# Two gather tables for the expert blocks: one with the first row alone, one with both

## The chip, the cores and the metric

The kernel runs on one core of one Trainium2 chip. The metric is device time in microseconds (us): the median of three runs for the kernel as it stands, and beside it the time of one profiled execution, from which all durations below come. Engines are named as in the profile: PE (TensorE), PEld (its weight loads), DVE (VectorE), ACT (ScalarE), POOL (GpSimd) and SP (SyncE, which here only issues DMAs). Everything is float32.

## The reference, cut to what matters

The input x has two rows (sequences) of 1024 tokens with 256 channels. Four residual steps follow each other: a conditioned state-space block with an MLP, a pooled mixture of 16 experts, a differential attention, and a top-1 mixture of 8 experts. The change touches the second:

```
h = pooled(x)               # per row: masked softmax pooling; every token reads tokens of its own row
logits = -|h - key_e|^2 + h . rw_e + rb_e          # 16 experts
topv, topi = top_k(logits, 4);  w = softmax(topv)
x = x + sum_k w_k * ( gelu(h @ w1[topi_k].T + b1) @ w2[topi_k].T + b2 )
```

Nothing in this step mixes tokens of the two rows. What a token needs for its experts is its own pooled row h (256 numbers) and its 16 expert weights (four of them not zero).

## The kernel before, in words

**Stages.** For each row b there are three pieces ahead of the experts:

- `mlp(b)` (lines 558 to 577): the MLP of the first residual step, 64 matmuls of 512 columns (L564) with a Gelu on ACT (L568) and 128 matmuls of 256 columns (L572). It leaves x in the tile `X[b]` and copies it to the DRAM table `acc[0]` (L575).
- `pooling(b)` (579 to 718): transposes of X (L585), scores (L594, Tanh L595, L599), two running maxima over 1024 tokens on DVE (L615, L616), exponentials on ACT (L653, L640, L664), the far part of the sums (L679) and a loop over eight tiles of tokens (L684, L685 on PE, L687 to L689 on DVE, L692 on ACT) that gives the pooled rows `pl`. Two DMAs write `pl` to the DRAM table `prow` (L694). Then the logits and the choice of the four experts (L702 to L718).
- `slots(s)` (743 to 860): sorts (token, expert) pairs into blocks of 256 slots that have one expert each. Counts are summed on PE (L758, L760), and one-hot matmuls (L832) turn slots into token numbers, which end in `idx[s]` (L860); `exi[s]` holds the expert of each block, `whose[s]` its mask. Within it, `weights_of(s)` (720 to 732) computes the expert weights of row s and writes them into the last 16 columns of `prow` (L730).

`slots(0)` sees row 0 alone. It fills up to eight blocks (`NB1`) with row 0's pairs, full blocks only. `slots(1)` sees both rows, leaves out what the first eight blocks hold, and fills the others. The program text has the order mlp(0), pooling(0), slots(0), mlp(1), pooling(1), slots(1), then the blocks.

**The expert blocks** (907 to 987). 36 blocks run always (`NB0`): eight of `s = 0`, then 28 of `s = 1`; further ones stand behind a condition. For each, `fetch` (910) loads the expert's weights, 2052 KB (L915), and its bias (L917) from SP, and POOL gathers 2 x 128 rows of `prow` into `gx` (L922). `turned` (928) transposes them (L933) and copies them to SBUF (L935). `block` (938) does 32 + 32 matmuls of 256 columns (L951 into `mm`, two PSUM banks; L963 into `o`) with a Gelu on ACT between them (L952), weighs the result (L959 to L966) and adds it into `acc` with an indirect DMA (L967). Weights have three buffers, `gx` four. The weights lie where the MLP weights lay (`block1.close()`, L895), so the first load waits for the last matmul of mlp(1).

**What sets the order.** The framework records all instructions with their dependencies, tile by tile, and orders each engine's queue when the kernel is built: it walks a model of the engines' times and takes, of what the model says is ready, the instruction that stands first in the program text. So mlp(1), which stands behind slots(0), fills the gaps that pooling(0) and slots(0) leave on PE. On the chip each queue then runs strictly in that order. A dependency on a DRAM table is kept for the range of it that an instruction names: the gather at L922 names all of `prow`, since the rows it takes are only known at run time.

```
            for h in range(2):
                pool.indirect_dma_start(
                    out=gx[:, h], out_offset=None, in_=prow,
                    in_offset=bass.IndirectOffsetOnAxis(ap=idx[s][:, 2 * j + h : 2 * j + h + 1], axis=0),
                )
```

`prow` has 2048 + 128 rows; the last 128 are zeros for slots that hold no pair (L889).

Of the kernel before, what the change touches and what calls it, by code (L numbers as in the profile page):

```python
# [11 lines left out]
F32 = mybir.dt.float32  # L12
# [7 lines left out]
P = 128  # L20
B, L, D = 2, 1024, 256
NT = L // P
NH, HP, NS = 8, 64, 64
DI = NH * HP
E0, F0, TOPK = 16, 1024, 4
# [50 lines left out]
def forward(ctx, tc, a):  # L76
    nc = tc.nc
# [3 lines left out]
    dram = ctx.enter_context(tc.tile_pool(name="dram", bufs=1, space=DRAM))  # L81
# [39 lines left out]

    ytab = dram.tile([B * L + P, 2 * D], F32, tag="ytab", name="ytab")

    prow = dram.tile([B * L + P, D + E0], F32, tag="prow", name="prow")
    acc = [dram.tile([B * L + P, D], F32, tag=f"acc{h}", name=f"acc{h}") for h in range(2)]


# [87 lines left out]
    with block0, tc.tile_pool(name="aps", bufs=2, space=PSUM, reuse_waits="tile") as ps:  # L215
# [21 lines left out]
        for b in range(B):  # L237
# [7 lines left out]
            for g in range(2):  # L245
                cols = slice(g * 512, (g + 1) * 512)
                p = ps.tile([P, 512], F32, tag=f"mm{b}", name="mm")
# [3 lines left out]
            for m in range(2):  # L251
                for g in range(2):
                    cols = slice(g * 512, (g + 1) * 512)
                    p = product(b, "Wg", both, m, cols)
                    act.activation(gated[b][:, m, cols], p, AF.Sigmoid, bias=C["bg"][:, m : m + 1])
                    pool.tensor_mul(gated[b][:, m, cols], gated[b][:, m, cols], xT[:, m, cols])
                    if m == 0:
                        for d in range(2):
                            p = ps.tile([P, 512], F32, tag=f"mm{b}", name="mm")
                            pe.matmul(  # L260
                                p, lhsT=C["Wn2"][:NS, d : d + 1].to_broadcast([NS, P]), rhs=h1[b][:, cols],
# [19 lines left out]
        for b in range(B):  # L281
            for g in range(2):
                cols = slice(g * 512, (g + 1) * 512)
                for m in range(2):
                    p = product(b, "Wsoma", [xTs[b][:, k] for k in range(2)], m, cols)
                    act.activation(soma[b][:, m, cols], p, AF.Gelu, bias=C["bsoma"][:, m : m + 1])
            for g in range(2):
                cols = slice(g * 512, (g + 1) * 512)
                for m in range(2):
                    p = product(b, "Wtemp", [ema[b][:, k] for k in range(2)], m, cols)  # L290
# [5 lines left out]
            for i in range(NT):  # L296
                p = ps.tile([P, D], F32, tag=f"o{b}", name="o")
                for k in range(2):
                    pe.matmul(
                        p, lhsT=soma[b][:, k, i * P : (i + 1) * P], rhs=WA["Wout"][:, k], start=k == 0, stop=k == 1  # L300
# [43 lines left out]
    with tc.tile_pool(name="b1", bufs=1, reuse_waits="tile") as bp:  # L344
# [4 lines left out]
        with tc.tile_pool(name="b2", bufs=2, reuse_waits="tile") as cp, tc.tile_pool(  # L349
            name="b3", bufs=1, reuse_waits="tile"  # L350
        ) as sp_, tc.tile_pool(
            name="bps", bufs=2, space=PSUM, reuse_waits="tile"
        ) as ps:
            for b in range(B):
# [27 lines left out]
                for g in range(2):  # L382
                    p = ps.tile([P, 512], F32, tag="mm", name="mm", bufs=3)
# [31 lines left out]
                t = taps(raw, C["bcw"])  # L415
# [3 lines left out]
                for c in range(4):  # L419
                    projected(xs[b][:, c], 512 + c * P)  # L420
                    t = taps(xs[b][:, c], C["cw"][:, c])
                    act.activation(xs[b][:, c, 3 : L + 3], t, AF.Silu, bias=C["cb"][:, c : c + 1])
                for i in range(NT):
                    p = ps.tile([P, 512], F32, tag="mm", name="mm", bufs=3)
                    for k in range(2):
                        pe.matmul(
                            p, lhsT=hT[:, k, i * P : (i + 1) * P], rhs=inp[:, k, 0:DI], start=k == 0, stop=k == 1
# [5 lines left out]
        with tc.tile_pool(name="b5", bufs=1, reuse_waits="tile") as sp, tc.tile_pool(  # L433
            name="b6", bufs=2, reuse_waits="tile"
        ) as tp, tc.tile_pool(name="bp1", bufs=2, space=PSUM, reuse_waits="tile") as p1, tc.tile_pool(
            name="bp2", bufs=1, space=PSUM, reuse_waits="tile"
# [6 lines left out]
            for b in range(B):  # L443
                vec.tensor_mul(av[b], dt[b], negA.unsqueeze(1).to_broadcast([P, NT, NH]))

                for dst, mat in ((ecs, K["U"]), (esuf, K["SL"]), (etot, ones)):
                    p = p2.tile([P, NT, NH], F32, tag="g", name="pg")
# [4 lines left out]
            for i, b in [(i, b) for i in range(NT) for b in range(B)]:  # L452
# [10 lines left out]
                for q in range(2):  # L463
                    p = p1.tile([P, 4, P], F32, tag="seg", name="seg")
# [114 lines left out]
    def pooling(b, cp, ps):  # L579
        xT = cp.tile([P, 2, L], F32, tag="xT", name="xT")  # L580
        for g in range(2):
            for k in range(2):
                t = ps.tile([P, 512], F32, tag="mm", name="tr")
# [5 lines left out]
        s, pre, suf = (cp.tile([P, L], F32, tag=t, name=t) for t in ("s", "pre", "suf"))  # L589
        for g in range(2):  # L590
            cols = slice(g * 512, (g + 1) * 512)
            p = ps.tile([P, 512], F32, tag="mm", name="mm")
# [5 lines left out]
            p = ps.tile([P, 512], F32, tag="mm", name="mm")  # L598
# [77 lines left out]
        pl = cp.tile([P, NT, DX], F32, tag="xT", name="pl")  # L676
        p = ps.tile([P, DX], F32, tag="mm", name="pf")
# [4 lines left out]
        for j in range(NT):  # L682
            p = ps.tile([P, DX], F32, tag="mm", name="po")
# [7 lines left out]
            n = b * NT + j  # L691
            act.activation(junk, pl[:, j, 0:D], AF.Square, accum_out=xsq[:, n : n + 1])  # L692
        for q in range(2):
            nc.sync.dma_start(  # L694
                out=prow[b * L + q * 512 : b * L + (q + 1) * 512, 0:D].rearrange("(i p) c -> p i c", p=P),
                in_=pl[:, 4 * q : 4 * q + 4, 0:D],
            )


        mine = slice(b * NT, (b + 1) * NT)  # L700
        lg_, gt_, eq_, rank_, wt_, ngt_ = lg[:, mine], gt[:, mine], eq[:, mine], rank[:, mine], wt[:, mine], ngt[:, mine]
# [18 lines left out]
    def weights_of(b):  # L720

        mine = slice(b * NT, (b + 1) * NT)
        wt_, ngt_ = wt[:, mine], ngt[:, mine]
        vec.tensor_sub(wt_, lg[:, mine], over_e(m8[:, mine, 0], half))
        act.activation(wt_, wt_, AF.Exp)
        vec.tensor_mul(wt_, wt_, gt[:, mine])
        vec.tensor_reduce(ngt_, wt_, AX.X, ALU.add)
        vec.reciprocal(ngt_, ngt_)
        vec.tensor_mul(wt_, wt_, over_e(ngt_, half))
        nc.sync.dma_start(  # L730
            out=prow[b * L : (b + 1) * L, D:].rearrange("(i p) c -> p i c", p=P), in_=wt_
        )

# [126 lines left out]
    with tc.tile_pool(name="cs", bufs=3, space=PSUM, reuse_waits="tile") as cs:  # L862
        with ExitStack() as c0:
            cp0 = c0.enter_context(tc.tile_pool(name="c0", bufs=1, reuse_waits="tile"))
            with tc.tile_pool(name="m1", bufs=2, side="right", reuse_waits="tile") as tp, tc.tile_pool(
                name="mps", bufs=2, space=PSUM, reuse_waits="tile"
            ) as ps:
                p = ps.tile([P, 512], F32, tag="mm", name="mm")
                for k in range(2):
                    pe.matmul(p[:, :E0], lhsT=ones, rhs=ksq[:, k], start=k == 0, stop=k == 1)  # L870
                vec.tensor_sub(rowb, R["rb"], p[:, :E0])
                h2 = [tp.tile([P, 2, L], F32, tag=f"h2{b}", name="h2", bufs=1) for b in range(B)]
                for b in range(B):
                    layernorm_T(h2[b], xa[b], C["ln2w"], C["ln2b"], tp, ps)
                for b in range(B):
                    x, wide = X[b][:, :, 0:D], [P, NT, D]
                    vec.tensor_add(x, x, xa[b])
                    vec.tensor_add(x, x, R["mb2"].unsqueeze(1).to_broadcast(wide))

                zero = tp.tile([P, 4 * D], F32, tag="zero", name="zero", bufs=1)  # L880
                pool.memset(zero, 0.0)
                for t, rows in ((acc[1], B * L),):
                    for q in range(rows // (4 * P)):
                        nc.sync.dma_start(
                            out=t[q * 4 * P : (q + 1) * 4 * P, :].rearrange("(i p) c -> p i c", p=P),
                            in_=zero.rearrange("p (i c) -> p i c", i=4),
                        )
                for t in (prow, ytab, *acc):
                    nc.sync.dma_start(out=t[B * L :, :], in_=zero[:, : t.shape[1]])  # L889
                mlp(0, tp, ps, h2[0])  # L890
                pooling(0, cp0, cs)
                with tc.tile_pool(name="d1", bufs=1, reuse_waits="tile") as cp:
                    slots(0, cp, cs)
                mlp(1, tp, ps, h2[1])
# [12 lines left out]
        with tc.tile_pool(name="fps", bufs=2, space=PSUM, reuse_waits="tile") as ps:  # L907
            got = {}

            def fetch(q):  # L910

                s, j = q
                e = nc.sync.value_load(exi[s][0:1, j : j + 1], min_val=0, max_val=E0 - 1)
                w = wpool.tile([P, FW], F32, tag="w", name="w")
                nc.sync.dma_start(out=w, in_=a["f0w"][bass.ds(e, 1)].rearrange("o p c -> p (o c)"))  # L915
                b2 = tp.tile([P, D], F32, tag="b2", name="b2", bufs=3)
                nc.sync.dma_start(  # L917
                    out=b2, in_=a["f0b2"][bass.ds(e, 1), :].rearrange("o c -> (o c)").partition_broadcast(P)
                )
                gx = tp.tile([P, 2, D + E0], F32, tag="gx", name="gx", bufs=4)  # L920
                for h in range(2):
                    pool.indirect_dma_start(  # L922
                        out=gx[:, h], out_offset=None, in_=prow,
                        in_offset=bass.IndirectOffsetOnAxis(ap=idx[s][:, 2 * j + h : 2 * j + h + 1], axis=0),
                    )
                got[q] = w, b2, gx
# [61 lines left out]
        with tc.tile_pool(name="d4", bufs=2, reuse_waits="tile") as tp:  # L988
            for b in range(B):
                nc.sync.dma_start(  # L990
                    out=X[b][:, :, 0:D], in_=acc[0][b * L : (b + 1) * L, :].rearrange("(i p) c -> p i c", p=P)
# [11 lines left out]
    with tc.tile_pool(name="e1", bufs=1, reuse_waits="tile") as cp, tc.tile_pool(  # L1003
        name="e2", bufs=2, reuse_waits="tile"
    ) as tp, tc.tile_pool(name="e3", bufs=1, reuse_waits="tile") as up_, tc.tile_pool(
        name="fs", bufs=2, space=PSUM, reuse_waits="tile"
    ) as p_s, tc.tile_pool(name="ft", bufs=1, space=PSUM, reuse_waits="tile") as p_t, tc.tile_pool(
        name="fm", bufs=2, space=PSUM, reuse_waits="tile"
# [255 lines left out]
    with tc.tile_pool(name="h1", bufs=1) as cp, tc.tile_pool(name="h2", bufs=2) as tp, tc.tile_pool(  # L1264
        name="hw", bufs=3
# [13 lines left out]
        with tc.tile_pool(name="i1", bufs=2) as up_, tc.tile_pool(name="i2", bufs=1) as ip, tc.tile_pool(  # L1279
            name="ips", bufs=2, space=PSUM  # L1280
        ) as ps:
            pg = ps.tile([P, N, E1], F32, tag="pg", name="pg", bufs=1)
            for b in range(B):
# [14 lines left out]
                for i in range(NT):  # L1298
                    p = ps.tile([P, D], F32, tag="o", name="o")
# [3 lines left out]
                for q in range(2):  # L1303
                    nc.sync.dma_start(
                        out=ytab[b * L + q * 512 : b * L + (q + 1) * 512, 0:D].rearrange("(i p) c -> p i c", p=P),
                        in_=yN[:, 4 * q : 4 * q + 4],
# [4 lines left out]
                for g in range(2):  # L1311
                    p = ps.tile([P, 512], F32, tag="o", name="o")
# [78 lines left out]
        with tc.tile_pool(name="jps", bufs=2, space=PSUM) as ps:  # L1391
# [27 lines left out]
            for e in range(E1):  # L1419
# [4 lines left out]
                gx, b2, dT = got.pop(e)  # L1424
                hh = tp.tile([P, 8, CAP], F32, tag="hh", name="hh")
                for f in range(8):
                    p = ps.tile([P, CAP], F32, tag="mm", name="mm", bufs=3)
# [5 lines left out]
                for s, n in parts:  # L1433
                    p = ps.tile([P, D], F32, tag="o", name="o")
                    for f in range(8):
# [7 lines left out]
                        out=a["out"].rearrange("b l c -> (b l) c"),  # L1443
                        out_offset=bass.IndirectOffsetOnAxis(ap=idx2[:n, col], axis=0),
                        in_=eo[:n], in_offset=None, bounds_check=B * L - 1, oob_is_err=False,
# [119 lines left out]
```

## Time and profile before

| | us |
|---|---|
| median of three runs (lowest, highest) | 1718.36 (1716.95, 1719.16) |
| the profiled execution, its own time | 1722.24 |
| its span in the trace | 1720.5 |
| busy in the span: PE, PEld, DVE, ACT, POOL | 1586.1, 1085.9, 783.1, 569.7, 350.0 |
| mean granted PE clock | 0.943 |

The page gives the busy time of each engine, then the span in 40 slices of 43 us; a digit is the busy share of a slice in tenths, 9 being 90% or more. In the row PEclk it is the clock that PE was granted, in tenths of the full one. Ends of matmuls are modelled, so a PE that counts as busy need not be at its peak. A table by stretches gives the same for stretches of one's own choice, with counts in brackets. A line of the waits names the instruction that waited, what ended its wait, the total, the number of times and the longest.

### The profile page before, as it was taken

Reading aid. Unit: us, or ns where it says so; the run is one execution under the profiler, and the core shown is the slowest. Engines: PE = TensorE matmul, PEld = TensorE weight load, DVE = VectorE, ACT = ScalarE, POOL = GpSimd, SP = SyncE. Lnnn points to the kernel's source line nnn. Section 1 sums busy time; section 2 is a strip of 40 time slices with the busy share of each in tenths; the row PEclk is TensorE's granted clock in tenths of the full one; section 3 lists DMA queues with packets and bytes.
Section 4 is the critical chain, followed back from the end, with each engine's and each line's share of the span. In section 5 each row is a group of like instructions: output and inputs, shape, how many; then the busy total and the mean of one; then the engine's idle time right before and its main releaser. Section 6 shows DMA issues by size and latency. Waiting matters only on the chain. (4 is left out here: it accounts for less than half of the span.)

```text
span 1720.5 us, 17699 instructions
## 1 busy us (share of the span) xinstructions
PE 1586.1 (92%) x6478; PEld 1085.9 (63%) x6478; DVE 783.1 (46%) x1854; ACT 569.7 (33%) x1146; POOL 350.0 (20%) x275
## 2 busy tenths in 40 slices
PE   8989999779997799999999999679999998859998
PEld 2444566546463688888888888535556554547775
DVE  6957666671645922222222222158755675231111
ACT  4556433221412122222222222116655564102221
POOL 2100355200000233333333332211000000022321
PEclk9989999979897799999999999889999998869999
DMA  5000000030006166666666665310000100443430
GB/s 197 1 1 0 1 1 0 1 114 25 25 2 233 53 191 195 195 196 195 194 194 194 194 194 175 67 52 1 1 1 1 50 0 1 165 134 122 163 107 11
DMA packets 54751, 156.79 MB, mean 91 GB/s; under 512 B 7819, under 2 KB 41867, under 8 KB 47488
## 3 DMA queue, kind: packets, MB, share of 16 engines
q1 hardware_dynamic: 38144, 128.86, 21.3%
q0 software_dynamic: 16512, 26.73, 7.5%
q8 instruction: 52, 0.85, 0.2%
q14 instruction: 43, 0.35, 0.1%
HBM read 130.74 MB, written 25.44 MB: 91 GB/s over the span
## 5 line engine op out<-in xcount | busy, mean ns | idle before, releaser
L952 ACT ACTIVATE hh<-mm,w 128x256 f32<-128x256 f32 x288 | 136.3, 473 | 398.7 <-PE mm L951 398.7
L951 PE MATMUL mm<-gT,w 128*128 128x256 f32 x1152 | 258.1, 382 | 0.8 <-DVE gT L935 0.8
L963 PE MATMUL o<-w,hh 128*128 128x256 f32 x1152 | 256.1, 379 | 0.0
L951 PEld LDWEIGHTS mm<-gT,w 128*128 128x128 f32 x1152 | 208.9, 191 | 42.9 <-ACT hh L952 2.6
L963 PEld LDWEIGHTS o<-w,hh 128*128 128x128 f32 x1152 | 215.7, 190 | 27.4
L967 POOL DMA_INDIRECT acc<-eo,idx x72 | 114.5, 1591 | 193.5 <-DVE wr L960 169.6
L922 POOL DMA_INDIRECT gx<-prow,idx x72 | 72.1, 1001 | 384.9 <-DVE nblk L778 224.8
L1151 PE MATMUL s<-kT,qz 128*128 128x512 f32 (+3 forms) x384 | 143.4, 495 | 5.2 <-DVE nm L1163 4.8
L935 DVE COPY gT<-t 128x512 f32<-128x512 f32 x36 | 24.9, 692 | 207.5 <-PE t L933 207.5
L1170 ACT ACTIVATE e<-e,nm 128x384 f32<-128x384 f32 (+7 forms) x128 | 98.7, 772 | 50.6 <-DVE nm L1163 49.5
L965 DVE TENSOR_TENSOR eo<-o,b 128x256 f32<-128x256 f32 x72 | 30.6, 425 | 180.2 <-PE o L963 180.2
L1163 DVE CUSTOM_DVE_ANT_0 e<-s,zneg 128x384 f32<-128x384 f32 (+7 forms) x128 | 95.3, 753 | 34.1 <-PE s L1151 29.8
L1151 PEld LDWEIGHTS s<-kT,qz 128*128 128x128 f32 x384 | 64.5, 190 | 48.0 <-issue 27.6
L1436 PE MATMUL o<-w,hh 128*128 128x256 f32 (+1 forms) x384 | 86.1, 382 | 0.0
L1436 PEld LDWEIGHTS o<-w,hh 128*128 128x128 f32 (+1 forms) x384 | 65.0, 172 | 18.3 <-issue 2.7
L1429 PE MATMUL mm<-dT,w 128*128 128x320 f32 x256 | 73.8, 448 | 0.5 <-DVE dT L193 0.5
L1430 ACT ACTIVATE hh<-mm,cols 128x320 f32<-128x320 f32 x64 | 33.7, 527 | 115.4 <-PE mm L1429 115.4
L1201 PE MATMUL po<-dT,vv 128*128 128x512 f32 (+3 forms) x192 | 68.3, 509 | 0.0
L1192 PEld LDWEIGHTS t<-consts,e 128*128 128x128 f32 x288 | 36.9, 149 | 45.3 <-ACT dT L193 15.8
L1090 POOL TENSOR_TENSOR sq<-qT 128x512 f32<-128x512 f32 x8 | 8.4, 1044 | 275.5 <-DVE qT L193 110.4
L1429 PEld LDWEIGHTS mm<-dT,w 128*128 128x128 f32 x256 | 49.6, 196 | 23.5 <-issue 4.7
L564 PE MATMUL mm<-h,wb 128*128 128x512 f32 x128 | 60.4, 618 | 0.4 <-ACT hh L568 0.4
(776 smaller groups left out, 2383.4 us busy)
## 6 DMA issues: line engine op xcount, KB each, us to landing
w<-in_f0w SPq DMA_DIRECT2D x36, 2052.0 KB, 8.7
w<-in_f1w SPq DMA_DIRECT2D x16, 1024.0 KB, 5.0
b<-in_f0b SPq DMA_DIRECT2D x36, 128.0 KB, 9.1
wb<-in_wb SPq DMA_DIRECT2D x1, 2560.0 KB, 17.5
X<-in_x SPq DMA_DIRECT2D x2, 1024.0 KB, 6.8
acc<-zero SPq DMA_DIRECT2D x4, 512.0 KB, 8.4
acc<-X SPq DMA_DIRECT2D x2, 1024.0 KB, 8.4
prow<-pl SPq DMA_DIRECT2D x4, 512.0 KB, 3.0
```

The source lines that it names most:

```text
L564: pe.matmul(p, lhsT=WB["m1"][:, k, f * P : (f + 1) * P], rhs=h2[:, k, g * 512 : (g + 1) * 512], start=k == 0, stop=k == 1,)
L922: pool.indirect_dma_start(out=gx[:, h], out_offset=None, in_=prow, in_offset=bass.IndirectOffsetOnAxis(ap=idx[s][:, 2 * j + h : 2 * j + h ...
L951: pe.matmul(p, lhsT=w1[:, k, f * P : (f + 1) * P], rhs=gT[:, k], start=k == 0, stop=k == 1)
L952: act.activation(hh[:, f], p, AF.Gelu, bias=fb[:, f : f + 1])
L963: pe.matmul(p, lhsT=hh[:, f, h * P : (h + 1) * P], rhs=w2[:, f], start=f == 0, stop=f == 7)
L967: pool.indirect_dma_start(out=acc[h], out_offset=bass.IndirectOffsetOnAxis(ap=idx[s][:, 2 * j + h : 2 * j + h + 1], axis=0), in_=eo, in_of ...
L1151: pe.matmul(t[:, s0:s1], lhsT=qz[b, c, i // 2][:, 2 * hp + j, (i % 2) * P : (i % 2 + 1) * P], rhs=kT[b][:, c, s0:s1], start=True, stop=True,)
L1163: vec.tensor_tensor_reduce(out=e[:, :n], in0=ss.pop((s, u))[:, :n], in1=zneg[:, L - n :], scale=-1.0, scalar=3e38, op0=ALU.add, op1=ALU.mi ...
L1170: act.activation(e[:, :n], e[:, :n], AF.Exp, bias=nm, scale=-1.0, accum_out=r)
L1201: pe.matmul(po[:, at:], lhsT=vv[b][:, q, c, hp : hp + 2].rearrange("p h d -> p (h d)"), rhs=dT[hp, q // 4][:, q % 4, at:], start=q == 0 an ...
L1429: pe.matmul(p, lhsT=w1[:, k, f * P : (f + 1) * P], rhs=dT[:, k], start=k == 0, stop=k == 1)
L1436: pe.matmul(p[:n], lhsT=hh[:, f, s * P : s * P + n], rhs=w2[:, f], start=f == 0, stop=f == 7)
```

## The change

`prow` becomes two tables of the same shape. Row 0's pooled rows and weights are written to both, row 1's only to the second. Rows 1024 to 2047 of the first are filled with zeros at the start of the stage. A block of `s = 0` gathers from the first, a block of `s = 1` from the second.

```diff
-    prow = dram.tile([B * L + P, D + E0], F32, tag="prow", name="prow")
+    prow = [dram.tile([B * L + P, D + E0], F32, tag=f"prow{s}", name=f"prow{s}") for s in range(2)]
...
         for q in range(2):
-            nc.sync.dma_start(
-                out=prow[b * L + q * 512 : b * L + (q + 1) * 512, 0:D].rearrange("(i p) c -> p i c", p=P),
-                in_=pl[:, 4 * q : 4 * q + 4, 0:D],
-            )
+            for t in prow[b:]:
+                nc.sync.dma_start(
+                    out=t[b * L + q * 512 : b * L + (q + 1) * 512, 0:D].rearrange("(i p) c -> p i c", p=P),
+                    in_=pl[:, 4 * q : 4 * q + 4, 0:D],
+                )
...
-        nc.sync.dma_start(
-            out=prow[b * L : (b + 1) * L, D:].rearrange("(i p) c -> p i c", p=P), in_=wt_
-        )
+        for t in prow[b:]:
+            nc.sync.dma_start(out=t[b * L : (b + 1) * L, D:].rearrange("(i p) c -> p i c", p=P), in_=wt_)
...
-                for t in (prow, ytab, *acc):
+                nc.sync.dma_start(
+                    out=prow[0][L : B * L, :].rearrange("(i p) c -> p i c", p=P),
+                    in_=zero[:, : D + E0].unsqueeze(1).to_broadcast([P, NT, D + E0]),
+                )
+                for t in (*prow, ytab, *acc):
                     nc.sync.dma_start(out=t[B * L :, :], in_=zero[:, : t.shape[1]])
...
                     pool.indirect_dma_start(
-                        out=gx[:, h], out_offset=None, in_=prow,
+                        out=gx[:, h], out_offset=None, in_=prow[s],
```

## The prediction

> **What bounds the kernel now.** I read the page first, the rows of slices, to see where the TensorE (PE) is not at work.
>
> ```profile
> span 1720.5 us, 17699 instructions
> ...
> PE 1586.1 (92%) x6478; PEld 1085.9 (63%) x6478; DVE 783.1 (46%) x1854; ACT 569.7 (33%) x1146; POOL 350.0 (20%) x275
> ...
> PE   8989999779997799999999999679999998859998
> PEclk9989999979897799999999999889999998869999
> ```
>
> A slice is 43 us. From slice 15 to slice 25 (about 606 to 1100 us) lie the 36 expert blocks, with PE full at full clock. Slices 13 and 14 (516 to 602 us) show 7 and 7, at a clock of 7 and 7: that is where row 1 is pooled and its slots are computed. A table by stretches resolves it; the columns are PE, PEld, DVE, ACT, POOL busy, then clock, DMA share and GB/s. The second group is the same work for row 0, with the MLP of row 1 beside it.
>
> ```profile
> 519.00:528.00 9.00, 7.40 (x34) 2.90 (x33) 3.05 (x6) 3.24 (x6) 0.00 (x0) 0.99 0.89 291
> 528.00:544.00 16.00, 6.50 (x22) 2.64 (x22) 14.77 (x29) 3.31 (x4) 0.00 (x0) 0.58 0.98 380
> 544.00:558.00 14.00, 13.86 (x31) 5.89 (x29) 5.78 (x22) 3.56 (x14) 0.00 (x0) 0.66 0.27 93
> 558.00:574.00 16.00, 3.65 (x9) 2.06 (x10) 14.16 (x66) 2.10 (x4) 5.14 (x5) 0.50 0.25 69
> 574.00:606.00 32.00, 32.00 (x198) 28.22 (x199) 29.71 (x101) 3.79 (x8) 7.66 (x9) 0.92 0.13 38
> ...
> 420.00:440.00 20.00, 20.00 (x77) 10.18 (x77) 11.58 (x19) 6.92 (x11) 0.00 (x0) 1.00 0.15 52
> 440.00:460.00 20.00, 18.81 (x55) 8.48 (x53) 12.14 (x35) 10.71 (x20) 0.00 (x0) 0.82 0.08 27
> 460.00:480.00 20.00, 19.96 (x72) 13.30 (x71) 15.69 (x88) 5.27 (x9) 0.00 (x0) 0.84 0.10 29
> ```
>
> Row 0's chain costs PE almost no idle time, because other matmuls fill it; row 1's chain leaves PE idle and at half clock. Next, the waits of PE from 519 to 606 us, to see what it waits for:
>
> ```profile
> PE pf L679 <- DVE wf L654: 9.5, 1, 9.5
> PE t L933 <- DMA gx<-prow,idx: 6.6, 2, 5.6
> PE mm L758 <- DVE gt L716: 5.1, 1, 5.1
> ```
>
> Last, why the blocks of row 0, whose slots were ready at 491.3 us (first idx of L860), start at 570.6. The page says that the first gather waited for DVE's nblk (L778). The gather's own line, in three stretches, says otherwise; its semaphore waits end one by one:
>
> ```profile
> L922 POOLq EVENT_SEMAPHORE  x1: 43/43/43, 552.6 to 552.6; - x1
> ...
> L922 POOLq EVENT_SEMAPHORE  x1: 43/43/43, 561.8 to 561.8; - x1
> ...
> L922 POOLq EVENT_SEMAPHORE  x2: 43/43/43, 566.7 to 566.8; - x2
> L922 POOL DMA_INDIRECT gx<-prow,idx x1: 1140/1140/1140, 567.6 to 567.6; - x1
> ```
>
> Row 1's two writes of pooled rows were issued at 549.25 and 558.81 (about 3.0 to landing) and its weights at 564.50 (2.1): they land at 552.3, 561.8 and 566.6. These are the gather's waits. It reads only rows of row 0, but names the whole table.
>
> **What the change takes away.** The first table holds no write of row 1 but zeros of about 354 us, so the eight gathers of row 0 need only writes of 454 to 475 us. The next thing that is late is the expert's weights: the first 2052 KB load is issued at 518.50, when the last L572 frees its memory, and takes 10.1 to land: 528.6. The second lands at 522.7 + 15.4 = 538.1, the third at 543.8. So block work can begin at 528.6 instead of 573.8.
>
> How much PE time is there to win? From 528.6 to 605.96, where the second block's L951 begins and everything is dense, are 77.4 us. The work done in them, at the pace of the dense stretch (32 matmuls of 256 columns in 6.90 us, 0.2156 each, in proportion to the columns): 16 of L679 with 273 columns, 3.7; 32 of L684 and L685, 7.4; L758 and L760, 0.9; 128 of L832 with 128 columns, 14.0; L856, 0.25; block 0 with its 64, 13.8; 8 transposes L933, 0.9. Together 40.8. So 36.6 us are lost: 21.7 idle (9.2 before L679, 5.1 before L758, 5.6 + 1.0 + 0.8 around the first transposes), the other 14.9 at half clock or in short waits, 7.1 of them in the pooling loop L684/L685 (14.5 us for 7.4 of work).
>
> Not all of it comes back, and the trace holds a model: row 0's chain beside mlp(1). From 433.6 to 518.0 us the same steps ran, filled with L564 and L572. Over the whole stage, 422.2 to 518.0, 95.8 us held 82.1 of work by the same counting (55.2 of mlp(1), 26.9 of row 0 and the transposes that open row 1), and 0.9 of the loss fell before 433.6; so 12.8 were lost, most in the loop, which the order did not fill there either and which fell to half clock at 453.9. Gain by the model: 36.6 - 12.8 = 23.8.
>
> **A rule against the row.** In that loop PE counts 18.81 of 20 us busy, yet its clock is 0.82 over the stretch, and single pairs take 1.27 instead of 0.73. The Trainium skill, "TensorE: Matmul & The Clock Gate", section "What's actually happening", says that one busy window of about 3.4 us brings the full clock. By the rule a filled PE would keep 1.00 and the gain would be up to 36.6; by the row it is 23.8. I take the row, and keep 36 as the upper end.
>
> **A rule that speaks against the change.** Row 1's chain needs Exp where the blocks need Gelu. Row 0's stage has six ACT_TABLE_LOAD (at 437, 440, 444, 447, 469, 470), row 1's only two (528, 562), each 1.28. So four are added. "ScalarE: Activation LUTs", section "What ACT_TABLE_LOAD costs", prices a switch at about 2.66 with a drain: 10.6 in all. The row shows the Exp of L640 starting at 445.15, 1.30 after its load at 443.85: 1.28 each, 5.1 in all. ACT is busy 2 to 4 of 16 us here, so they cost PE only where both mm banks of a block (0.86 us of PE each) are full meanwhile. Bounds 0 and 10.6; I take 1.
>
> **What it adds.** One more zero fill of rows 1024 to 2047 (1.1 MB, 3.7 us at the 302 GB/s of that stretch) at about 354 us, when X of row 1 (issued 349.01, 7.1 to landing, 356.1) feeds L877 at 356.7. It is queued behind it on SP; bounds 0 and 3.7, taken 0. If that cover were gone, PE's wait for hn (11.5 us before 360.3) would grow. The row 0 copies into the second table: two 512 KB writes at 454 and a 64 KB one at 473, on a DMA system busy 0.08 to 0.10; SP spends 0.38 per issue, three issues, 1.1 us, and nothing on SP is due before 518.5. They land by 480; their first reader is block 8. One more pad row write (136 KB): nothing. All zero on the path.
>
> **What it moves.** Twelve gathers of about 1 us go earlier on POOL, which is idle for 224.8 us until 567.6: free. SP: the fourth weight load must wait for block 0's last L963 and can be queued ahead of or behind row 1's writes into the second table (L694 at 549, L730 at 564.5). Either way something is held: behind L730, it comes at 565 rather than about 550, while block 3 is due only after three blocks and some 26 us of row 1's matmuls, near 595; ahead of them, the table waits for a block's end, and nobody reads it before block 8. DVE gets about 2 us of block work (gT 0.69, eo 0.43, mine and wr) per block into a chain that is 14.77 of 16 us busy: row 1's chain grows by some 5 us. It is done at 606.0 now and is needed by block 8, which cannot start before 528.6 + 8 x 14.27 + about 26 of row 1's own matmuls (40.8 less block 0) = 669. So it has 60 us of slack.
>
> **Sum.** 23.8 - 1 (tables) - 0.5 (weights later than the plan expects) = about 22.5. The profiled execution took 1722.24 with a span of 1720.5, which would become 1698; the runs shown lie at a median of 1718.36, 3.9 lower, so 1718.4 - 22.5 = 1696.
>
> **The rivals.** (1) Fuller filling: the order puts block matmuls into the loop and the clock holds. For: the blocks' L951 and L832 alternate without a gap from 582 to 606. Against: the loop at 449 to 462. Gain 30 to 36, time 1685. (2) Stalls eat half: the order, fixed beforehand, puts the first L951 ahead of row 1's L594 and L599, which then stand behind a load that lands at 528.6 (up to 7 us), and each Exp stops L951 for 1 to 2 us (up to 6). Gain 5 to 15, time 1708. (3) The slower side: the order gives the eight blocks precedence, and row 1's chain runs behind them. From 643 on (528.6 + 114) its 36.6 us of loss would stand uncovered as before, with four table loads (5.1) and the early copies on top: 1723. It decides once row 1's chain ends after about 669, 60 us later than now. Against it: in row 0's stage the chain went first and mlp(1) filled. (4) Nothing changes: another wait holds the first gather. The waits above name three writes and no fourth, so this is small: 1718.
>
> **How the numbers follow.** About 0.2% (3.4 us) is what a measurement of this kernel can tell from no change. The forecast, gain 15 to 30, gets 0.62; rival 1, 0.14; rival 2, 0.13; rival 4, 0.05; rival 3, 0.06. Faster: 0.62 + 0.14 + 0.12 = 0.88; same 0.06; slower 0.06. Range: from 1685 (the most that I give to filling) to 1709 (most of rival 2).
>
> **What would show it.** The gather's waits end before 518, the first L951 starts near 529, PE's idle time before L679 and L758 goes (from 14.6 to under 3), the row-1 stretch has six table loads, the loop L684/L685 still shows pairs of 1.27, the last L963 ends near 1082 instead of 1105, and all stages behind it keep their lengths. I am wrong if L951 starts after 545, if PE waits for w or for idx of row 1 at block 8, or if the clock between 530 and 600 stays under 0.8.

## The result, and the profile after

| | before | changed |
|---|---|---|
| median, us (lowest to highest) | 1718.11 (1716.95 to 1719.16) | 1690.3 (1686.68 to 1694.06) |
| profiled execution, its own time | 1722.24 | 1690.81 |
| its span | 1720.5 | 1689.0 |

Each median is of four runs. The medians differ by 27.8 us, where the prediction said 22.5 (1696, range 1685 to 1709). The ratio on record is 0.9829, 95% interval 0.9813 to 0.9846; taken by itself it would mean 29.4 us. A later set of six runs gave 1690.9, ratio 0.9843 (0.9817 to 0.9869). The changed kernel's time varies more from execution to execution than these medians differ (1687.93 to 1700.2 in that set). Part of it is the PE clock in one loop of each row, which differs between executions of one program (experiments 5, 6 and 10).

The page of the changed kernel. A slice is 42 us now; slices 13 and 14 are 507 to 591 us.

```profile
span 1689.0 us, 17707 instructions
...
PE 1574.0 (93%) x6478; PEld 1080.2 (64%) x6478; DVE 781.4 (46%) x1854; ACT 572.0 (34%) x1148; POOL 350.4 (21%) x275
...
PE   8989999859999999999999999689999998859997
PEclk9989999979999899999999999789999999869999
```

Slices 13 and 14 show PE at 9 and 9, where it had 7 and 7, and a clock of 9 and 8 instead of 7 and 7. The table by stretches (columns: length, busy time of PE, PEld, DVE, ACT, POOL, then clock, DMA share, GB/s) shows where:

```profile
440.00:460.00 20.00, 18.81 (x63) 8.89 (x62) 14.89 (x45) 11.87 (x24) 0.00 (x0) 1.00 0.16 53
...
519.00:528.00 9.00, 7.69 (x40) 4.60 (x40) 6.61 (x8) 2.21 (x4) 2.83 (x3) 1.00 0.99 345
528.00:544.00 16.00, 15.82 (x66) 9.87 (x64) 13.28 (x39) 9.72 (x15) 1.49 (x1) 1.00 0.87 358
544.00:558.00 14.00, 14.00 (x27) 6.89 (x27) 6.00 (x27) 3.24 (x14) 0.13 (x1) 0.51 0.29 78
558.00:574.00 16.00, 16.00 (x78) 13.84 (x77) 15.04 (x65) 5.38 (x10) 5.09 (x4) 1.00 0.60 177
574.00:606.00 32.00, 31.82 (x207) 28.24 (x206) 28.62 (x93) 3.79 (x8) 6.19 (x5) 1.00 0.33 90
```

The two stretches that were nearly empty (6.50 of 16 us, 3.65 of 16) are full, at clock 1.00. Row 1's pooling loop, in 544 to 558, is at 0.51: 27 matmul instructions in 14 us. In this execution row 0's loop (440 to 460) has clock 1.00, where it had 0.82.

What PE waits for between 515 and 700 us (the instruction, what ended its wait, total, times, longest), in place of the 9.5, 6.6 and 5.1 us of before:

```profile
PE mm L956 <- DMA w<-in_f0w: 1.0, 1, 1.0
PE mm L600 <- ACT th L596: 0.7, 2, 0.3
PE pf L680 <- DVE wf L655: 0.2, 1, 0.2
PE mm L833 <- DVE at__3267 L830: 0.2, 1, 0.2
```

And the gather's own line between 460 and 490 us: its semaphore waits and the first gathers.

```profile
L927 POOLq EVENT_SEMAPHORE  x4: 17/43/22168, 461.9 to 487.5; - x4
L927 POOL DMA_INDIRECT gx<-prow,idx x2: 962/1051/1140, 488.4 to 489.8; - x2
```

The first gather starts at 488.4 instead of 567.6. What is late next is the weight load, as the prediction said: the first block matmul (L956) runs at 524.31, after 0.97 us of waiting for `w`. (Lines from 125 on have moved, most by one to five: L956 was L951, L968 was L963, L573 was L572, L680 was L679, L685 and L686 were L684 and L685.)

**Where the span's 31.5 us went.** I split it at starts of matmuls. Up to the first L573 the changed kernel is 1.8 later (382.6 against 380.8). From there to mlp(1)'s last L573 it takes 131.3 instead of 137.2 (-5.9). From there to the last L968 it takes 561.6 (513.9 to 1075.5) instead of 586.7 (518.0 to 1104.7): -25.1. All that follows takes 613.5 instead of 615.8 (-2.3). The third term is the change's. The second is clock, in row 0's pooling loop and the eight L565 behind it. PE's instructions stand in the same sequence of lines there in all profiles compared (before, changed, and experiments 1 to 4), and this stretch took 131.2 to 131.3 in the three profiles in which that loop kept its clock (two of the changed kernel, one of experiment 3) and 137.1 to 137.2 in the five in which it fell to half clock at the fifth tile. The fourth is variation between executions: another profile of the kernel before has 612.2 there, another of the changed kernel 612.0.

### The profile page after: what moved, and what is told of

Its sections match the earlier page's. It is cut to its first block, busy times and chain, and to the rows that moved or that the text cites. A ratio compares the mean times of both kernels' runs of the same rounds, so it can differ in the third digit from the quotient of the medians.

```text
span 1689.0 us, 17707 instructions
## 1 busy us (share of the span) xinstructions
PE 1574.0 (93%) x6478; PEld 1080.2 (64%) x6478; DVE 781.4 (46%) x1854; ACT 572.0 (34%) x1148; POOL 350.4 (21%) x275
## 5 line engine op out<-in xcount | busy, mean ns | idle before, releaser
L956 PE MATMUL mm<-gT,w 128*128 128x256 f32 x1152 | 257.0, 380 | 1.0 <-DMA w<-in_f0w 1.0
L968 PE MATMUL o<-w,hh 128*128 128x256 f32 x1152 | 257.3, 381 | 0.0
L968 PEld LDWEIGHTS o<-w,hh 128*128 128x128 f32 x1152 | 216.9, 191 | 29.4 <-issue 1.2
L956 PEld LDWEIGHTS mm<-gT,w 128*128 128x128 f32 x1152 | 206.9, 189 | 41.9 <-ACT hh L957 5.0
L565 PE MATMUL mm<-h,wb 128*128 128x512 f32 x128 | 58.9, 604 | 0.4 <-ACT hh L569 0.4
## 6 DMA issues: line engine op xcount, KB each, us to landing
wb<-in_wb SPq DMA_DIRECT2D x1, 2560.0 KB, 17.6
```

What stands on the lines that cost most here:

```text
L565: pe.matmul(p, lhsT=WB["m1"][:, k, f * P : (f + 1) * P], rhs=h2[:, k, g * 512 : (g + 1) * 512], start=k == 0, stop=k == 1,)
L956: pe.matmul(p, lhsT=w1[:, k, f * P : (f + 1) * P], rhs=gT[:, k], start=k == 0, stop=k == 1)
L968: pe.matmul(p, lhsT=hh[:, f, h * P : (h + 1) * P], rhs=w2[:, f], start=f == 0, stop=f == 7)
```

## The experiments

All have the changed kernel as their base unless the edit says otherwise. Kernels of one group ran on the same chip with the kernel before beside them.

**1. Everything of the change but the gather's table.** Two tables are kept, filled and written as in the change, and all blocks read the second.

```diff
-                        out=gx[:, h], out_offset=None, in_=prow[s],
+                        out=gx[:, h], out_offset=None, in_=prow[1],
```

> All of the change but one argument: both tables are written and the zero fill is there, but the first eight blocks gather from the second table, which waits for row 1. Theory (the wait of the row-0 gathers for row 1's writes is the whole gain): the gain goes, first L956 near 574, time 1718 to 1721, the upper end if the zero fill costs 1 to 2 us. Rival A (part of the gain is in the order of the engines' queues or in the split of the writes, not in the wait): 1700 to 1712. Rival B (chance of the clock in the pooling loops gives several us): the row-0 loop L685/L686 runs at 0.73 or at 1.27 per pair, and the time differs by 4 to 6 us accordingly.

Measured: 1720.21 (20 runs) beside 1720.8 for the kernel before, ratio 0.9999 (0.9989 to 1.0009). The first L956 ran at 578.5, in a profile in which mlp(1) ended 4.6 later than in that of the kernel before. PE's waits are those of before:

```profile
PE pf L680 <- DVE wf L655: 9.5, 1, 9.5
PE t L938 <- DMA gx<-prow,idx: 6.7, 2, 5.8
PE mm L759 <- DVE gt L718: 5.1, 1, 5.1
```

The zero fill, the three doubled writes and the second pad row cost nothing beyond the interval (some 1.7 us either way), and earn nothing: the whole gain hangs on which table the gather names. Since the order of the queues is built from the same dependency, this takes back the wait and the new order together, and can't tell them apart. Both pooling loops fell to half clock here, as in the kernel before, so rival B doesn't bear on it.

**2 and 3. How many blocks need to be free?** The first table for one or for two blocks; the others of row 0 read the second table and so wait for row 1, though their data are row 0's.

```diff
-                        out=gx[:, h], out_offset=None, in_=prow[s],
+                        out=gx[:, h], out_offset=None, in_=prow[0 if s == 0 and j < 1 else 1],
```

(and `j < 2` in the second kernel)

> Only the first expert block gathers from the first table; the other seven of row 0 gather from the second, which is complete at about 567. Theory (the blocks are cover for PE until row 1's table lands): between about 524 and 567 PE has 43 us, row 1's own matmuls take some 19 of them, so one block (13.8 us) leaves about 10 us uncovered; time 1697 to 1703, two thirds of the gain kept. Rival (each of the eight blocks brings its share): one eighth of the gain, 1713 to 1716.

> The first two blocks gather from the first table, six from the second. Theory: two blocks (27.7 us) fill the 24 us that row 1's matmuls leave up to 567, so nearly all of the gain is there: 1689 to 1693. Rival (each block brings its share): a quarter of the gain, 1709 to 1713.

| blocks that read the first table | median, us | ratio (95%) | last L573 to last L968 in the profile |
|---|---|---|---|
| 0 (experiment 1) | 1720.21 | 0.9999 (0.9989 to 1.0009) | 586.9 |
| 1 | 1713.79 | 0.9959 (0.9944 to 0.9975) | 576.7 |
| 2 | 1695.4 | 0.9867 (0.9845 to 0.9889) | 566.6 |
| 8 (the change) | 1690.3 and 1690.9 | 0.9829, 0.9843 | 561.6, 561.7 |

With one block the time lies in the rival's range (1713 to 1716), and my number was missed by more than 10 us; with two it is 2.4 above my range and 14 below the rival's (1709 to 1713), so equal shares are out. The one-block kernel's waits on PE, then POOL's first gather from the second table and SP's two issues around it (start, length, instruction):

```profile
PE t L938 <- DMA gx<-prow,idx: 12.7, 2, 11.9
PE mm L956 <- DVE gT L940: 1.5, 1, 1.5
PE mm L759 <- DVE gt L718: 1.4, 1, 1.4
```

```profile
575.57 1.07 POOL L927 DMA_INDIRECT gx<-prow,idx  x1 [8.45 <-DMA prow<-wt]
```

```profile
564.25 0.36 SPq L920 DMA_DIRECT2D w<-in_f0w  x1
568.99 0.36 SPq L733 DMA_DIRECT2D prow<-wt  x1
```

One block covers row 1's two earlier waits (the 9.5 us before L680 is not among PE's waits any more, L759's is 1.4), but then PE is out of work until row 1's table is whole. That takes longer than in the kernel before: counted from mlp(1)'s last matmul, 52.7 us (522.0 to 574.7) instead of 48.6, for the last 64 KB of it (`wt`) are issued behind a 2 MB weight load and take 5.7 us to land, where they took 2.1. So PE waits 12.7 us before block 1's transposes, twice the 6.6 of before; the first eight L956 after it then took 3.78, where eight take 1.89 at full clock. All waits on PE in this stage sum to 17.6 us, 6.0 less than the 23.6 of experiment 1's kernel. With two blocks the same wait is

```profile
PE t L938 <- DMA gx<-prow,idx: 4.1, 1, 4.1
```

and nearly all of the gain is there. So the gain is not a share per block: it is what it takes to keep PE at work until row 1's table has landed and been gathered from (578.5 us with one block, 574.0 with two), and two blocks beside row 1's own matmuls almost do. In the last column the one-block profile kept its clock in row 1's loop and the others did not (some 5 us), so by the medians the first block brings less (6.4) and the second more (18.4).

**4. The zero fill out of the way of X.** In the changed kernel DVE waited 1.3 us at L878 for row 1's `X`, landing 9.0 after issue instead of 7.1. Rows 1024 to 2047 of the first table get row 0's data, late, in place of the zero fill.

```diff
-                nc.sync.dma_start(
-                    out=prow[0][L : B * L, :].rearrange("(i p) c -> p i c", p=P),
-                    in_=zero[:, : D + E0].unsqueeze(1).to_broadcast([P, NT, D + E0]),
-                )
...
-            for t in prow[b:]:
+            for t, r in [(t, b) for t in prow[b:]] + ([(prow[0], 1)] if b == 0 else []):
                 nc.sync.dma_start(
-                    out=t[b * L + q * 512 : b * L + (q + 1) * 512, 0:D].rearrange("(i p) c -> p i c", p=P),
+                    out=t[r * L + q * 512 : r * L + (q + 1) * 512, 0:D].rearrange("(i p) c -> p i c", p=P),
```

(and the same at L733)

> The rows of the first table that nobody reads are filled with copies of row 0's rows at about 455 and 470 us, when DMA is nearly idle, in place of the zero fill at 355. Theory: the zero fill delays the landing of X of row 1 and with it L878 (1.3 us of DVE idle, mlp(0)'s L573 starts 1.8 us later than in the kernel before); without it L573 starts near 380.8 and the time is 1 to 2 us below the changed kernel's: 1688 to 1690. Rival: the delay is the order of the queues, not the fill, and nothing is gained: 1690 to 1691.

Measured: 1693.24 (1688.41 to 1699.09, five runs), ratio 0.9846 (0.9821 to 0.9872). Row 1's `X` landed in 6.4 and L878 did not wait, but the time is not below the changed kernel's. That decides little: L573 started at 379.3, 3.3 earlier than in the changed kernel's profile, and then row 0's loop fell to half clock and took 5.8 more; in runs that spread over 10.7 us, one or two can't be seen. Nor is the fill shown to be the cause of the late landing. In the seven profiles with the fill `X` landed in 7.8 to 9.1 (8.5 on average), in the five without it in 6.4 to 8.4 (7.6), and experiments 1 and 2, with 7.8, had no wait at L878, while experiment 7, with no fill and 8.4, waited 0.7. What makes `X` late stays open.

**5. The changed kernel once more,** for its variation.

> The changed kernel itself, run again beside the kernels below and with a profile of its own. Theory (in each pooling loop L685/L686 PE's clock falls to half some 5 us after the loop begins, in most executions but not all, at about 5.8 us a time): time 1688 to 1694 with a spread of 5 us or more between runs, and the profile shows each of the two loops either at 0.73 per pair throughout (10 us) or at 1.27 from the fourth tile on (14.5 us). Rival (the row-0 loop keeps the full clock because of the changed order): the row-0 loop again runs at 0.73 throughout and the row-1 loop at 1.27.

Measured: 1690.9 (1687.93 to 1700.2). Its profile has row 0's loop at full clock and row 1's at half, as the first, which is what the rival said; experiment 10 speaks against it.

**6. The loop that falls to half clock.** For each token tile the pooling loop issues L685 (128 rows contracted) and L686 (16 rows). Here L686 contracts over 128 rows too; rows 16 to 127 of its operands are zero, so the sums stay the same. No table and no gather is touched. (Besides, `fT` gets a buffer of its own where it shared that of `th`; what this alone does was not run.)

```diff
-        fs = cp.tile([NF, DX], F32, tag="fs", name="fs")
-        vec.tensor_copy(fs, p[:NF])
+        fs = cp.tile([P, DX], F32, tag="fs", name="fs")
+        pool.memset(fs, 0.0)
+        vec.tensor_copy(fs[:NF], p[:NF])
...
-        fT = cp.tile([NS, L], F32, tag="th", name="fT")[:NF].rearrange("p (t j) -> p t j", j=P)
+        fT = cp.tile([P, L], F32, tag="fT", name="fT").rearrange("p (t j) -> p t j", j=P)
```

(and `farT`, `sel` and `seen` likewise on 128 partitions)

> The changed kernel with the second matmul of the pooling loop (L686) contracted over 128 partitions, of which rows 16 to 127 are zeros, in place of 16. The work on PE by columns is the same; fT, seen and farT are computed on 128 partitions. Theory (PE loses its clock because the 16-row matmuls and their weight loads leave it too little active in this loop): both loops stay at the full clock, each takes 10 us or less, and the time falls by 4 to 12 us, to 1680 to 1688. Rival (what counts is that the loop waits for DVE and for its weight loads between matmuls, whatever the rows): the loops still fall to 1.27 per pair, time unchanged within 2 us.

Measured: **1677.05** (1676.61 to 1680.21, five runs), ratio 0.9754 (0.9734 to 0.9774): below both kernels, below the range of my theory, and the fastest version of this study. Its stretches; then the second matmul of the loop between 430 and 575 us (busy and mean ns, then idle time before and what ended it), which is L687 in this kernel, and the changed kernel's L686; then three lines of row 0's loop, here and in the changed kernel (start, length, instruction):

```profile
440.00:460.00 20.00, 18.81 (x69) 11.19 (x68) 16.18 (x54) 12.88 (x26) 0.00 (x0) 1.00 0.21 73
528.00:544.00 16.00, 15.51 (x68) 10.75 (x67) 13.26 (x42) 9.55 (x19) 1.62 (x1) 1.00 0.82 314
544.00:558.00 14.00, 13.76 (x66) 11.51 (x65) 13.04 (x67) 6.76 (x16) 2.37 (x2) 1.00 0.73 229
```

```profile
L687 PE MATMUL po<-fs,fT 128*128 128x273 f32 x32 | 9.7, 396 | 0.0
...
L687 PEld LDWEIGHTS po<-fs,fT 128*128 128x128 f32 x32 | 6.0, 190 | 1.6 <-DVE fs L683 0.4
```

```profile
L686 PE MATMUL po<-fs,fT 16*128 16x273 f32 x32 | 13.6, 522 | 0.0
...
L686 PEld LDWEIGHTS po<-fs,fT 16*128 16x128 f32 x32 | 5.7, 216 | 6.6 <-issue 6.0 <-DVE fs L682 0.4
```

```profile
452.18 0.62 PE L686 MATMUL po<-X,ET 128*128 128x273 f32 x2
452.64 0.62 PE L687 MATMUL po<-fs,fT 128*128 128x273 f32 x2
453.10 0.62 PE L686 MATMUL po<-X,ET 128*128 128x273 f32 x2
...
451.89 0.73 PE L685 MATMUL po<-X,ET 128*128 128x273 f32 x2
452.55 0.72 PE L686 MATMUL po<-fs,fT 16*128 16x273 f32 x2
453.20 0.73 PE L685 MATMUL po<-X,ET 128*128 128x273 f32 x2
```

Each matmul of the program stands as two instructions in the trace (x2), a pair. The clock is 1.00 in both loops, and there is more than the clock: pairs now start every 0.46 us, where 16-row and 128-row pairs alternated every 0.655 at full clock and every 1.21 at half. Of the idle time of PEld ahead of the second matmul, 6.6 us over 32 loads with 6.0 of "issue", 1.6 is left. So both matmuls of the loop were held up when 16 and 128 rows alternated, while PE counted as busy throughout. DVE's work per tile is the same in both kernels, so it did not set the pace.

Between the first profile of the changed kernel and this one lie 13.9 us: 2.4 in mlp(1)'s stretch with row 0's loop, 8.2 in the stage with row 1's, and 3.3 before and behind them, where the loop does not run.

**7. Experiments 4 and 6 together.**

> Both edits together: no zero fill at 355 us, and 128 rows in the pooling loop. If each works by itself: 1 to 2 us below the 128-row kernel, 1679 to 1687. If neither does: 1688 to 1693.

Measured: 1684.43 (1678.08 to 1686.3, five runs), ratio 0.9789 (0.9767 to 0.9811). The number lies in the first range, but only because experiment 6 came out lower than that range assumed: it is 7.4 above 6 alone, not 1 to 2 below. The profile, of the fastest of the five runs, shows no loss (the stage takes 553.4 as in 6, with both loops at full clock); the three slower runs have a granted clock of 0.958 over the whole span against 0.960 and 0.962, and no profile of one was kept. So the fill moved gains nothing that is shown, and even with the 128-row loop a spread of 8 us can remain.

**8. The kernel before with the 128-row loop.** Against experiment 6 it gives the two tables alone, with both loops at full clock in both.

> The kernel before with one table, and with the second matmul of the pooling loop over 128 rows, so that no chance of the clock is left in either loop. Theory (the change by itself is worth the wait of the row-0 gathers, whatever the clock does in the loops): both loops at 0.46 to 0.62 per pair, time 1700 to 1706, so 23 to 29 us above the 128-row kernel with two tables (1677.05). Rival (part of the 27.8 us was clock that happened to be granted to the changed kernel): 1694 to 1698, only 17 to 21 above.

Measured: 1705.63 (1703.42 to 1709.82, six runs), ratio 0.9925 (0.9908 to 0.9942), in the range of the theory. Both loops ran at 0.46 per pair. PE's waits (L934 is L933 of the kernel before, L759 its L758):

```profile
PE pf L679 <- DVE wf L654: 9.6, 1, 9.6
PE t L934 <- DMA gx<-prow,idx: 6.6, 2, 5.6
PE mm L759 <- DVE gt L717: 5.1, 1, 5.1
```

The waits of row 1 are untouched by the faster loop. The step from here to experiment 6 is 28.6 us between the medians, which were taken on two chips; the ratios, each to the kernel before on the same chip, give 0.9754 / 0.9925 = 0.983. In the profiles the stage from mlp(1)'s last matmul to the blocks' last takes 579.6 here (510.3 to 1089.9) and 553.4 there (511.0 to 1064.4): 26.2 us. All waits of PE in the stage sum to 23.6 here and 2.5 there, so 21.1 are waits, and some five are what PE ran at half clock just behind the long ones (16 L679 took 5.31 here and 3.85 there, the first eight L952 3.78, where eight take 1.89 there). That is the worth of the change with the loops' clock held.

**9 and 10. Each kernel once more,** for the loops.

> The kernel before, one more profile. If the row-0 loop's clock is a matter of chance, its pairs may run at 0.73 throughout here (mlp(1) ends some 6 us earlier); if the place of the loop in time decides, they fall to 1.27 as in the first profile.

> The changed kernel, one more profile. If chance decides the clock of the row-0 loop, it may fall to 1.27 here (time 1694 to 1700); if not, it stays at 0.73 as in two profiles so far (1687 to 1691). The row-1 loop falls to 1.27 by either.

Measured: 1718.41 and 1691.65, one run each. In the kernel before both loops fell to half clock again. In the changed one row 0's fell only at its sixth tile and row 1's not at all (start, length, instruction; the fifth and sixth tile of row 0, then the last of row 1):

```profile
458.42 0.73 PE L685 MATMUL po<-X,ET 128*128 128x273 f32 x2
459.73 1.16 PE L685 MATMUL po<-X,ET 128*128 128x273 f32 x2
```

```profile
556.90 0.73 PE L685 MATMUL po<-X,ET 128*128 128x273 f32 x2
```

while the first profile of the same kernel has, in row 1's loop, its fourth and fifth tile as

```profile
543.48 0.73 PE L685 MATMUL po<-X,ET 128*128 128x273 f32 x2
...
545.20 1.28 PE L685 MATMUL po<-X,ET 128*128 128x273 f32 x2
```

In experiment 10's profile the stage took 555.8 (522.1 to 1077.9), 6 less than with a fallen loop. Which loop falls, and when, differs between executions of one kernel. Of the 18 loops with 16 rows in the nine profiles here 13 fell; of the six with 128 rows in three profiles none.

## Why the prediction was right, and where it was off

**The mechanism and its place.** Right. One wait, that of the gathers on three writes of row 1, held eight blocks; it moved to 488, the weight load became the next late thing, and block matmuls filled row 1's chain. Load and first L956 came 10.4 us after mlp(1)'s last matmul; the step said 10.6. Experiment 1 shows that the table which the gather names is all of it, and experiments 2 and 3 that the idle time up to the landing of row 1's table is what the blocks fill.

**The sum for the stage.** Predicted about 22.5 (the terms as written add up to 22.3), measured 25.1 in the profile and 26.2 with the loops' clock held. The terms:

- Idle: the 21.7 us went, as counted; 2.1 us of short waits are left.
- ACT table loads: the term was 1, for four added loads. Two were added (the page counts 1148 ACT instructions instead of 1146):

```profile
531.08 1.28 ACT L654 ACT_TABLE_LOAD   x1
532.70 1.28 ACT L957 ACT_TABLE_LOAD   x1
535.35 1.28 ACT L641 ACT_TABLE_LOAD   x1 [0.51 <-DVE farT L659]
559.45 1.28 ACT L957 ACT_TABLE_LOAD   x1
```

  No wait of PE on ACT stands beside them (the 0.7 us for `th` lie before the first). I had counted row 0's six loads and expected the same of row 1; the order grouped row 1's Exps more closely. By the 2.66 per switch of the Trainium skill ("ScalarE: Activation LUTs", section "What ACT_TABLE_LOAD costs") the two would be 5.3; the rows show 1.28 each, with the next activation 1.30 after the start of its load, and hidden behind PE's work.
- Weights later than the plan expects: the term was 0.5. PE's only wait for `w` is the 1.0 at the first block, already in the 10.4.
- What the model left in the stage, 12.8: about right with a fallen loop. Row 1's loop lost 7.5 (539.10 to 554.85, with 8.3 of work), the 16 L968 behind it 1.6, and the short waits 2.1: 11.2 together. The three terms were too dark by 2.8 us in all.
- What the 7.1 us lost in the loop are: the prediction put them to half clock or short waits. Experiment 6 splits them: row 0's loop of 16 pairs takes 14.5 us fallen, 10.1 at full clock, and 7.8 with 128 rows. So some 4.4 are clock, and nearly all of the rest is the pace of alternating rows.

**The rule and the row.** I took the row (a busy loop at half clock) over the Trainium skill's rule ("TensorE: Matmul & The Clock Gate", section "What's actually happening"), and for the first profile that held: 0.51 in 544 to 558, with no gap in PE's record. But it is not a property of this loop that can be counted on: in experiment 10 it kept 1.00, and the stage was 586.7 - 555.8 = 30.9 us shorter than before, between the row's 23.8 and the rule's 36.6. The row showed one outcome of two, and I put it into the sum as certain. And busy is not dense: by experiment 6 the loop issues a pair every 0.655 us at full clock where 0.46 can be had. That the sparser issue is what the clock answers to is consistent with all profiles here, but the one edit that made it denser also changed the rows and the buffer of `fT`, so it is not shown apart from these.

**From the span to the medians.** 5.7 us of difference remain between 1696 and 1690.3. The stage gives 2.6. The rest I can only place, not prove: row 0's loop, which the change does not touch, ran at full clock in two of the three profiles of the changed kernel and fell in both of the kernel before; the 5.9 us in the first profile are that. Whether the change makes this likelier (by moving the loop in time, or by what runs around it) or three profiles are luck, stays open: in experiments 1 and 4 both loops fell, in 2 row 0's alone, in 3 row 1's alone. This part of the gain the prediction did not foresee.

**What it adds, and what it moves.** Taken as zero, and zero within 1.7 us by experiment 1. The zero fill had bounds of 0 and 3.7: in the first two profiles of the changed kernel PE's wait for `hn` was 12.9 and 13.0 instead of 11.5, about 1.4 more, and L573 started later. That the fill does it is not shown: the wait was 11.7 in experiments 1 and 2, which have the fill, and 12.3 and 12.4 in experiments 8 and 7, which do not. The prediction left open how the fourth weight load would be queued; it went ahead of row 1's `wt` (560.23 and 564.43). That held `wt` no later than before (564.50), but it landed in 6.6 instead of 2.1, which no term had. Nobody reads it before block 8. With one block free, experiment 2, somebody does, and it costs.

**The rivals.** (1) A clock that holds: in row 1's loop it did in one of three profiles of the changed kernel, and in both loops of every profile with 128 rows. It did not come from filling: in the changed kernel no block matmul stands between the last six tiles of that loop. (2) Stalls that eat half: no; PE's waits after 515 sum to 2.1 us. (3) Row 1's chain last: no; its last `idx` came at 601.0, and block 8's transposes ran at 669.3. (4) Another wait: no.

## What to carry to other kernels

In this framework a gather with run-time indices depends on everything that is written to the tensor it names; when the rows it can take are known to be a part, give it a tensor of its own that only that part's writers touch, and check that the copies cost nothing by making them without using them. What a freed wait is worth is the idle time it covers up to the next thing that is late, so ask how much independent work is needed to reach that point: here two blocks of eight brought 25 of 30 us (against experiment 1). And read a busy row together with its pace: PE counted as full in a loop that started a pair every 0.655 us where every 0.46 was to be had, and mending that loop was worth another 13 us by the medians, of which the profiles place some 10 in the stretches with the loop.

## What the runs showed of the hardware that I had not expected

- Alternating 16-row and 128-row contractions, PE issued a pair of 273-column matmuls every 0.655 us at full clock; with both at 128 rows, of which 112 are zeros, every 0.46. More multiplications took less time.
- The same loop in the same program kept full clock in one execution and fell to half in another, at different tiles, with PE counted as busy in the tiles before it. With 128 rows both loops kept a pair every 0.46 us in all three profiles.
- A 64 KB write took 5.7 to 6.8 us to land when a 2 MB load had been issued some 4 to 5 us before it (four profiles), 2.1 in the kernel before.
- Four ACT_TABLE_LOADs at 1.28 us each lie beside block matmuls without a PE wait on ACT.
